# A modulation product moved out of the first attention unit, with its arithmetic spread over later groups

## The chip, the cores and the metric

The kernel runs on one core of a Trainium2 chip. The metric is the device time of one execution in microseconds; lower is better. The engines are named as in the profile: PE is TensorE (matrix products), with PEld for its weight loads; DVE is VectorE, ACT is ScalarE, POOL is GpSimd, and SP is the engine whose queue issues most of the DMAs. Each engine works through its own queue in program order and waits on semaphores for the others.

## The reference

It is one transformer block with adaptive layer norm. A small vector `c` per batch element yields six modulation rows, the attention is an ordinary softmax attention with 16 heads over 1024 tokens and 8 batch elements, and the second half is a mixture of eight experts, each of which picks its 512 best tokens.

```python
mod = (_silu(L0_c) @ L0_wmod).reshape(8, 6, 1, 256)
sa, ca, ga, sb, cb, gb = (mod[:, i] for i in range(6))
ga = (2 * (ga >= 0) - 1) * jnp.maximum(jnp.abs(ga), 0.25)
gb = (2 * (gb >= 0) - 1) * jnp.maximum(jnp.abs(gb), 0.25)
h = _layernorm(x) * (1 + ca) + sa
x = x + ga * attention(h, w_qkv, w_o)
h = _layernorm(x) * (1 + cb) + sb
x = x + gb * experts(h, router_w, router_b, w1, b1, w2, b2)
```

The change touches only `ga`, `sb`, `cb` and `gb`: they are needed late, at the end of the first batch element's attention, while `sa` and `ca` are needed at once.

## The kernel before

The attention is cut into 128 units (`NSU`): one unit is a batch element, a pair of heads and half of the queries. A unit has four groups, so the program runs through groups g = -1, 0, 1, 2, ... and unit u begins at group 4u. In every group PE computes two score products of the current unit into PSUM tiles `s` (L393); ACT copies them into SBUF tiles `p` (L402) and DVE keeps a running maximum `top` of them (L410). In the first group of the next unit (`gm == 0`) the finished maximum is turned: PE transposes `top` into the PSUM tile `tt` (`max_turn`, L420), DVE reduces it and splits it in three bfloat16 parts (`split_max`, L428 to L438), PE turns these into `pn` (`max_rows`, L444), ACT copies that to `nr` (L449), and a group later PE spreads it over all rows as `less` (`max_spread`, L457). DVE then subtracts it from the scores (L460), eight times a unit, ACT takes the exponentials (L463), PE multiplies with the values (L473, tile `av`), and POOL sums the exponentials for the denominators (L493, L496).

Everything else hangs as tasks at a group and a place in it. `at(g, where, f, *args)` registers a task, `run(g, where)` issues it. The order of the places in a group is: "load", "turn", the turn of the maximum, the score products and their copies, "post" (in a unit's first group it comes here, in other groups later), subtractions, "add" and "sum", maxima and the remaining subtractions, "m1", exponentials, products with the values (in a unit's first group `max_rows` stands among them or in their place), "pool", "m2". The schedule is manual: this program order is each engine's order.

In the first groups the query, key and value products (`qk_task` L352 with copies L357 and L363, `v_task` L373 with copy L378) are tasks at "m1". Their PSUM buffers come from `bank`, which hands out a list written by hand before it falls back on the single buffer "mm":

```python
    early = [(ps_s, "s")] * 2 + [(ps_m, "mm"), (ps_av, "av")] + [
        (ps_b, "less"), (ps_m, "mm"), (ps_av, "av")
    ] * 4
```

The buffer "less" also serves `tt` and `less`, "mm" also serves `pn`, and "av" the products with the values. Each of the three has one buffer, so a new tile in it waits until the tile before it has been read.

The modulation rows are made by `mod_rows(i)` for i = 0 and 1, each with four matrix products (L228) into a tile `pr` from `bank` and a copy by ACT into the tile `mrow` (L231), which has eight rows. The call with i = 1 goes on with the arithmetic on DVE (one addition, L234, and four operations for each of the two gates, L238 to L242) and stores the rows to DRAM by two DMAs on SP's queue (L243, L244). The calls are tasks at "m2" of groups 2 and 3. The tile `mrow` lies in the buffer "rb", of which there is one; its next taker is the spread denominator `rb` (`den_spread`), first loaded in group 21 for POOL's multiplication in group 22 (L558). The stored rows are first read from DRAM in group 30 (`gates`) and in group 80 (`out_load`).

Of the kernel before, what the change touches and what calls it, by code (L numbers as in the profile page):

```python
# [28 lines left out]
F32 = mybir.dt.float32  # L29
# [5 lines left out]
ALU = mybir.AluOpType  # L35
# [9 lines left out]
def adaln_block(  # L45
# [15 lines left out]
    nc = tc.nc  # L61
    B, S, D = x.shape
# [66 lines left out]
    small = attn.enter_context(tc.tile_pool(name="small", bufs=4))  # L129
# [68 lines left out]
    mod_row = []  # L198
# [22 lines left out]
    def mod_rows(i):  # L221

        if i == 0:
            mod_row.append(work.tile([B, 4 * D], F32, tag="rb", name="mrow", bufs=1))
        mrow = mod_row[0]
        pr = bank([B, 2 * D], f"pr{i}")
        for k in range(KC):
            nc.tensor.matmul(  # L228
                pr, sT[:, k, :], wm[1 + i][:, k, :], start=(k == 0), stop=(k == KC - 1)
            )  # L230
        nc.scalar.copy(mrow[:, 2 * i * D : (2 * i + 2) * D], pr)  # L231
        if i == 0:
            return
        nc.vector.tensor_scalar_add(mrow[:, 2 * D : 3 * D], mrow[:, 2 * D : 3 * D], 1.0)  # L234
        for i in (0, 3):
            g = mrow[:, i * D : (i + 1) * D]
            sign = small.tile([B, D], F32, tag="ox", name=f"sign{i}", bufs=3)
            nc.vector.tensor_scalar(sign, g, 0.0, 2.0, op0=ALU.is_ge, op1=ALU.mult)  # L238
            size = small.tile([B, D], F32, tag="at", name=f"size{i}", bufs=2)
            nc.vector.scalar_tensor_tensor(size, g, -1.0, g, op0=ALU.mult, op1=ALU.max)  # L240
            nc.vector.tensor_scalar_max(size, size, 0.25)
            nc.vector.scalar_tensor_tensor(g, sign, -1.0, size, op0=ALU.add, op1=ALU.mult)  # L242
        nc.sync.dma_start(mod_d, mrow[:, : 3 * D])  # L243
        nc.sync.dma_start(gb_d, mrow[:, 3 * D :])  # L244

# [5 lines left out]
    def at(g, where, f, *args):  # L251
        steps.setdefault((g, where), []).append((f, args))
# [13 lines left out]
    def bank(shape, name):  # L266
        pool, tag = early.pop(0) if early else (ps_m, "mm")
        return pool.tile(shape, F32, tag=tag, name=name)
# [490 lines left out]
    for b in range(B):  # L759
# [17 lines left out]
        if b + 1 < B:  # L777
            for t in range(NT):
                g = 64 * (b + 1) + 18 + 8 * t
# [17 lines left out]
    for b in range(B):  # L797
        at(64 * b + 30, "load", gates, b)
    for i in range(2):
        at(2 + i, "m2", mod_rows, i)  # L800
    at(4 * NSU - 2, "load", last_mods)
    at(4 * NSU - 6, "load", last_load)
    at(4 * NSU + 4, "load", last_load_den, 0)
# [3 lines left out]
    with tc.manual_schedule():  # L807
# [15 lines left out]
        g = -1  # L823
# [172 lines left out]
    with tc.tile_pool(name="search", bufs=2) as se, tc.tile_pool(  # L996
        name="pos", bufs=1
    ) as po_, tc.tile_pool(name="se_ps", bufs=2, space=PSUM) as sps, tc.tile_pool(
        name="pos_ps", bufs=1, space=PSUM
    ) as pps:  # L1000
        for dst, pattern, mult in (
# [3 lines left out]
            i = po_.tile(list(dst.shape), I32, name=f"i_{dst.name}")  # L1005
# [324 lines left out]
```

## Time and profile before

| | us |
|---|---|
| median of 3 runs | 3397.42 (3396.98 to 3397.81) |
| profiled execution | 3399.97 |
| its span, first to last instruction | 3398.3 |
| PE busy | 3316.2 (98% of the span) |
| DVE busy | 2723.2 (80%) |
| POOL busy | 2702.0 (80%) |
| ACT busy | 2465.8 (73%) |
| mean granted PE clock | 0.987 |

The span is what the trace covers; the profiled execution's own time has 1.67 us more around it. Times in the views are microseconds from the start of the span. In the trace groups 2, 3, 4, 8, 12 and 16 begin on PE at 29.05, 36.33, 43.62, 68.84, 89.95 and 111.60 us. A regular unit thus takes about 21 to 22 us, and the attention takes most of the span. A line of a timeline gives the start, the duration, the engine, the source line and operation, what it writes and reads, how many instructions are merged into the line, and in brackets the idle time of the engine before it with whom it waited for.

### The profile page before, as it was taken

The page shows a single profiled execution, that of the slowest core. Times are in us where ns is not written, and L with a number is a line of the kernel's source. Part 1 is how long each engine was busy: PE and PEld are TensorE (multiplying, and loading weights), DVE is VectorE, ACT ScalarE, POOL GpSimd, SP SyncE. Part 2 cuts the span into 40 slices and gives each one's busy share as a digit, 9 for nine tenths or more (in the row PEclk, how much of TensorE's full clock was granted, in tenths as well). Part 3 has the DMA queues.
Part 4 walks back from the last instruction along what each step waited for, and adds up shares of the span by engine and source line. Part 5 has one row for each costly group of instructions (what it writes and reads, how often), then busy time and mean ns, then how long its engine had stood idle before and what let it go on. Part 6 is the DMA issues. An engine that isn't in the chain of part 4 may idle for free. (4 is left out here: it accounts for less than half of the span.)

```text
span 3398.3 us, 60059 instructions
## 1 busy us (share of the span) xinstructions
PE 3316.2 (98%) x23647; PEld 1345.2 (40%) x23647; DVE 2723.2 (80%) x3391; ACT 2465.8 (73%) x3069; POOL 2702.0 (80%) x1611
## 2 busy tenths in 40 slices
PE   8999999999999999999999999999999999985998
PEld 3333333333333333333333333333333333334666
DVE  6898888888888888888888888888888888876332
ACT  5888887778777877778777787878777787760221
POOL 2899888988898888989898888988898888881333
PEclk9999999999999999999999999999999999996999
DMA  4020012111121112111121112111211112124342
GB/s 82 14 48 30 26 48 53 45 46 53 45 63 42 47 53 56 43 46 51 48 59 42 47 53 56 49 40 51 61 46 48 42 51 60 51 76 140 105 102 44
DMA packets 184110, 183.66 MB, mean 54 GB/s; under 512 B 49148, under 2 KB 161292, under 8 KB 183700
## 3 DMA queue, kind: packets, MB, share of 16 engines
q1 hardware_dynamic: 167860, 158.44, 16.9%
q0 software_dynamic: 7168, 12.72, 1.9%
q10 hardware_dynamic: 8800, 8.68, 0.8%
q8 instruction: 185, 3.03, 0.4%
q14 instruction: 97, 0.79, 0.1%
HBM read 126.01 MB, written 62.16 MB: 55 GB/s over the span
## 5 line engine op out<-in xcount | busy, mean ns | idle before, releaser
L496 POOL TENSOR_TENSOR acc<-acc,p 128x1024 f32<-128x1024 f32 x764 | 1816.3, 2377 | 89.8 <-ACT p L463 42.3
L402 ACT COPY p<-s 128x1024 f32<-128x1024 f32 x1024 | 990.4, 1016 | 332.7 <-PE s L393 311.4
L460 DVE TENSOR_TENSOR p<-p,less 128x1024 f32<-128x1024 f32 x1024 | 1211.3, 1214 | 8.7 <-PE less L457 3.7
L410 DVE TENSOR_TENSOR top<-top,s 128x1024 f32<-128x1024 f32 x768 | 934.2, 1216 | 134.6 <-ACT p L402 120.1
L463 ACT ACTIVATE p<-p 128x1024 f32<-128x1024 f32 x1024 | 1025.4, 1052 | 1.4 <-DVE rd L695 1.0
L393 PE MATMUL s<-qk,qk 64*128 64x512 f32 (+1 forms) x6144 | 999.1, 603 | 3.2 <-DVE top L410 3.2
L473 PE MATMUL av<-p,v 128*64 128x512 f32 x4096 | 995.5, 596 | 1.6 <-ACT p L463 1.4
L352 PE MATMUL pq<-hT,wq 128*64 128x512 f32 x2048 | 497.3, 607 | 0.7 <-ACT hT L304 0.7
L393 PEld LDWEIGHTS s<-qk,qk 64*128 64x128 f32 (+1 forms) x6144 | 315.5, 151 | 418.1 <-issue 232.2
L473 PEld LDWEIGHTS av<-p,v 128*64 128x64 f32 x4096 | 270.6, 137 | 487.1 <-issue 387.6
L493 POOL TENSOR_TENSOR acc<-p,p 128x1024 f32<-128x1024 f32 x128 | 304.7, 2380 | 61.5 <-ACT p L463 61.5
L428 DVE TENSOR_REDUCE tt<-tt 128x8 f32<-128x1024 f32 x128 | 157.7, 1232 | 176.2 <-PE tt L420 176.2
L352 PEld LDWEIGHTS pq<-hT,wq 128*64 128x64 f32 x2048 | 124.9, 136 | 350.0 <-issue 219.4
L373 PE MATMUL pv<-wq,hT 128*64 128x256 f32 x2048 | 249.8, 386 | 0.0
L630 POOL TENSOR_TENSOR ox<-ox,at 128x256 f32<-128x256 f32 x56 | 40.6, 725 | 253.1 <-DVE at L625 253.1
L614 PE MATMUL po<-wo,ot 128*64 128x256 f32 x1792 | 202.9, 379 | 0.0
L373 PEld LDWEIGHTS pv<-wq,hT 128*64 128x64 f32 x2048 | 136.0, 137 | 156.8 <-issue 58.3
L410 DVE TENSOR_TENSOR top<-p,s 128x1024 f32<-128x1024 f32 x128 | 154.8, 1209 | 46.1 <-ACT p L402 42.8
L614 PEld LDWEIGHTS po<-wo,ot 128*64 128x64 f32 x1792 | 128.6, 137 | 88.7 <-issue 32.0
L558 POOL TENSOR_TENSOR oT<-oT,rb 128x1024 f32<-128x1024 f32 x63 | 150.1, 2382 | 0.0
L357 ACT ACTIVATE qk<-pq 128x512 f32<-128x512 f32 x128 | 76.5, 598 | 94.9 <-PE pq L352 94.9
L1264 POOL DMA_INDIRECT out_dram<-eo,tok x32 | 53.8, 1680 | 115.0 <-DMA out_dram<-eo,tok 61.4
(192 smaller groups left out, 2237.8 us busy)
## 6 DMA issues: line engine op xcount, KB each, us to landing
rb<-rden_d SPq DMA_DIRECT2D x126, 256.0 KB
oT_d<-oT SPq DMA_DIRECT2D x60, 512.0 KB
ot<-oT_d SPq DMA_DIRECT2D x56, 512.0 KB
rows_d<-gb_d SPq DMA_DIRECT2D x8, 1024.0 KB
w<-in_L_ffn_w_dram SPq DMA_DIRECT2D x8, 1024.0 KB
w<-in_L_ffn_w_dram ACTq DMA_DIRECT2D x8, 1024.0 KB
rows_d<-row SPq DMA_DIRECT2D x62, 132.0 KB
lnx<-in_L_attn_inputs_dram SPq DMA_DIRECT2D x28, 256.0 KB
```

Of the source, the lines that this page charges most:

```text
L352: nc.tensor.matmul(pq[m * N : (m + 1) * N, :], wq_of(k, a, 2 * p + m), hTs[b][:, k, sl], start=(k == 0), stop=(k == KC - 1),)
L373: nc.tensor.matmul(pv[m * N : (m + 1) * N, i, :], hTs[b][:, k, t0 : t0 + N], wq_of(k, 2, 4 * g, 4), start=(k == 0), stop=(k == KC - 1),)
L393: nc.tensor.matmul(ps[k : k + n, j, :], kt[r, c * P + k : c * P + k + n], qt[r, h * QB : (h + 1) * QB], start=True, stop=True,)
L402: nc.scalar.copy(probs[u, c], ps)
L410: nc.vector.tensor_tensor(tops[u], probs[u, 0] if c == 1 else tops[u], ps, ALU.max)
L428: nc.vector.tensor_reduce(nm[:, 0, :], tt.rearrange("p r q k -> p q r k"), AX.XY, ALU.max, negate=True)
L460: nc.vector.tensor_tensor(probs[u, c], probs[u, c], less[u], ALU.add)
L463: nc.scalar.activation(probs[u, c], probs[u, c], AF.Exp)
L473: nc.tensor.matmul(avs[u][j * N : (j + 1) * N, :], v[:, c, hh * N : (hh + 1) * N], pT[:, j, :], start=(c == 0), stop=(c == NT - 1),)
L493: nc.gpsimd.tensor_tensor(sums[u], pts[0], pts[1], ALU.add)
L496: nc.gpsimd.tensor_tensor(sums[u], sums[u], pt, ALU.add)
L614: nc.tensor.matmul(po[m * N : (m + 1) * N, :], ot[:, p, m * N : (m + 1) * N], wo[:, p, :], start=(p == 0), stop=(p == NP - 1),)
```

## The change

The two calls of `mod_rows` move from "m2" of groups 2 and 3 to group 4, the first group of the second unit: the call with i = 0 to "m1" (before `max_rows`), the one with i = 1 to "m2" (after it). The arithmetic of the gates becomes `mod_gate`, called at "post" of groups 8 and 12, and the addition with the two stores becomes `mod_store`, called at "post" of group 16. All of these are first groups of a unit, where "post" stands ahead of the subtractions and maxima. The number of instructions stays the same.

```diff
@@ mod_rows
         nc.scalar.copy(mrow[:, 2 * i * D : (2 * i + 2) * D], pr)
-        if i == 0:
-            return
+
+    def mod_gate(i):
+        g = mod_row[0][:, i * D : (i + 1) * D]
+        sign = small.tile([B, D], F32, tag="ox", name=f"sign{i}", bufs=3)
+        nc.vector.tensor_scalar(sign, g, 0.0, 2.0, op0=ALU.is_ge, op1=ALU.mult)
+        size = small.tile([B, D], F32, tag="at", name=f"size{i}", bufs=2)
+        nc.vector.scalar_tensor_tensor(size, g, -1.0, g, op0=ALU.mult, op1=ALU.max)
+        nc.vector.tensor_scalar_max(size, size, 0.25)
+        nc.vector.scalar_tensor_tensor(g, sign, -1.0, size, op0=ALU.add, op1=ALU.mult)
+
+    def mod_store():
+        mrow = mod_row[0]
         nc.vector.tensor_scalar_add(mrow[:, 2 * D : 3 * D], mrow[:, 2 * D : 3 * D], 1.0)
-        for i in (0, 3):
-            g = mrow[:, i * D : (i + 1) * D]
-            sign = small.tile([B, D], F32, tag="ox", name=f"sign{i}", bufs=3)
-            nc.vector.tensor_scalar(sign, g, 0.0, 2.0, op0=ALU.is_ge, op1=ALU.mult)
-            size = small.tile([B, D], F32, tag="at", name=f"size{i}", bufs=2)
-            nc.vector.scalar_tensor_tensor(size, g, -1.0, g, op0=ALU.mult, op1=ALU.max)
-            nc.vector.tensor_scalar_max(size, size, 0.25)
-            nc.vector.scalar_tensor_tensor(g, sign, -1.0, size, op0=ALU.add, op1=ALU.mult)
         nc.sync.dma_start(mod_d, mrow[:, : 3 * D])
         nc.sync.dma_start(gb_d, mrow[:, 3 * D :])
@@ the tasks
     for i in range(2):
-        at(2 + i, "m2", mod_rows, i)
+        at(4, ("m1", "m2")[i], mod_rows, i)
+        at(8 + 4 * i, "post", mod_gate, 3 * i)
+    at(16, "post", mod_store)
```

## The prediction

> **What bounds the kernel now.** I read the page first: TensorE (PE) is busy for 98% of the span and its slices are flat until the tail, so a change pays only where it takes time off PE's path. The chain that ended last reaches back only over the last microseconds and says nothing of the start.
>
> ```profile
> span 3398.3 us, 60059 instructions
> PE 3316.2 (98%) x23647; PEld 1345.2 (40%) x23647; DVE 2723.2 (80%) x3391; ACT 2465.8 (73%) x3069; POOL 2702.0 (80%) x1611
> ```
>
> Second, the windows view over the first units (columns: window, length, busy us of PE, PEld, DVE, ACT, POOL, granted clock, DMA share, GB/s). PE is full from 20 to 44 us, has a hole in 44 to 49, and runs at half clock from there to about 55.3. Unit 2 (69 to 90) is full again.
>
> ```profile
> 36.00:44.00 8.00, 8.00 (x57) 2.80 (x58) 2.44 (x2) 3.96 (x6) 0.00 (x0) 1.00 0.00 1
> 44.00:49.00 5.00, 2.10 (x20) 0.79 (x16) 4.42 (x13) 2.23 (x3) 0.00 (x0) 1.00 0.05 10
> 49.00:51.00 2.00, 1.02 (x11) 0.81 (x13) 1.31 (x3) 0.58 (x1) 0.00 (x0) 0.50 0.00 0
> 51.00:53.00 2.00, 2.00 (x8) 1.00 (x6) 1.74 (x2) 0.03 (x1) 0.00 (x0) 0.50 0.00 0
> 53.00:55.00 2.00, 2.00 (x6) 0.35 (x6) 1.60 (x2) 1.30 (x2) 0.00 (x0) 0.50 0.00 0
> 69.00:90.00 21.00, 21.00 (x132) 6.67 (x130) 19.22 (x20) 17.87 (x22) 16.46 (x8) 1.00 0.00 1
> ```
>
> Third, PE's timeline there (start, length, operation, idle before and its releaser). Both products of the modulation rows (pr) are on a full PE. After the turn of the running maximum (tt) and two scores, PE waits 3.19 us for VectorE's `parts`.
>
> ```profile
> 34.52 1.88 PE L228 MATMUL pr<-wm,sT 128*8 128x512 f32 x4
> ...
> 39.99 1.89 PE L352 MATMUL pq<-hT,wq 128*64 128x512 f32 x8
> 41.80 1.88 PE L228 MATMUL pr<-wm,sT 128*8 128x512 f32 x4
> 43.62 0.71 PE L420 MATMUL tt<-ident,top 64*128 64x64 f32 x16
> 44.17 1.93 PE L393 MATMUL s<-qk,qk 64*128 64x512 f32 x8
> 49.30 0.64 PE L444 MATMUL pn<-ident_b,parts 128*64 128x128 bf16 x8 [3.19 <-DVE parts L438]
> 50.62 0.61 PE L457 MATMUL less<-nr,three 64*128 64x512 bf16 x2 [0.68 <-ACT nr L449]
> 51.00 3.64 PE L393 MATMUL s<-qk,qk 64*128 64x512 f32 x8
> ```
>
> Fourth, VectorE's timeline says why `parts` is late: the modulation arithmetic stands before the reduction in its queue and holds it until 47.14.
>
> ```profile
> 44.33 0.28 DVE L234 TENSOR_SCALAR mrow<-mrow 8x256 f32<-8x256 f32 x1 [3.26 <-ACT mrow L231]
> ...
> 46.80 0.41 DVE L242 SCALAR_TENSOR_TENSOR mrow<-sign,size 8x256 f32<-8x256 f32 x1
> 47.14 1.21 DVE L428 TENSOR_REDUCE tt<-tt 128x8 f32<-128x1024 f32 x1
> ```
>
> **The change, part by part.** I follow the edges on the profiled clock until tt of group 8 (68.84 before), where the pipeline is in its regular step.
>
> *Products out of groups 2 and 3.* Each costs PE its pitch: 34.52 to 36.33 and 41.80 to 43.62, 3.63 us together. ScalarE (about 3.1 us of work in such a group) and VectorE (2.54) have room in the 5.45 us left, so tt could start at 39.99.
>
> *A new wait there.* `bank` hands out a written list of PSUM buffers; two calls less before the third group's tasks move each later taker on by one. The last v product takes "av", and the query product of group 3 takes "less", the buffer that tt needs. Its copy by ScalarE ran 41.92 to 42.52; 1.81 earlier that is 40.11 to 40.71, and tt starts at 40.77, not 39.99. Behind tt in PE's queue stand the scores. That is 2.85 us earlier than before.
>
> *Arithmetic out of VectorE's way.* The reduction starts 0.75 after tt (68.84 to 69.59 in the next unit), at 41.52, and `parts` is done 2.16 later (47.14 to 49.30): 43.68.
>
> *Products into group 4.* PE: scores 41.32 to 43.18 (0.55 and 1.86 after, as at 43.62), the first product from 43.18, ended 45.06. It lies in "mm", which pn wants next, so pn waits for ScalarE's copy (0.05 and 0.58, the rows of L231): 45.75. So only some 0.5 us of the first product fill the wait for `parts`; the rest and the copy delay pn by 2.07. It is still 3.55 earlier than 49.30. The second product ("av", free since group 3) starts a warm pn pitch later (0.23, from 72.16 to 72.39): 45.98 to 47.80. It covers the copy nr (done about 46.8). So less starts at 47.80 (50.62 before). Its own copy of 0.58 on ScalarE ends at about 48.4, before the next scores are there at 49.0.
>
> *Unit 1 after that.* VectorE starts subtracting 0.43 after less (73.35 to 73.78): 48.23. Its eight subtractions and six maxima took 16.11 us without gaps in unit 2 (73.78 to 89.89), and 17.53 in unit 1 (51.26 to 68.79), where the half clock made scores late. With the clock up they end at 64.34, and tt starts at 64.40. PE's own work of 14.8 us from 47.80, with its waits for score buffers, ends near 64.2. Gain at group 8: 68.84 - 64.40 = 4.44 us.
>
> *The clock.* The row: 3.19 us of idle PE was followed by a granted 0.50 until about 55.3, and scores took 3.64 instead of 1.88. The two waits I add (0.78 and 0.75) are nearest to the 0.53 us one at 64.12, in a stretch granted 1.00, so I take no drop. The other bound: one drop like that of before, priced by its rows as 1.76 (scores), 0.69 (v, pitch 2.47 against 1.78) and 0.47 (pn, less), 2.9 us in all.
>
> The Trainium skill, "TensorE: Matmul & The Clock Gate", Part 1, puts the drop after an idle window of about 3.4 us that runs free of the kernel. Read strictly it would have spared the 3.19 us gap, and the regained clock time (estimate 1.4 us of the gain, 17.53 - 16.11) would not exist, so the gain at group 8 would be 3.0; the row shows the drop, and the row decides.
>
> *Gates into groups 8 and 12.* Four operations each, 1.30 us by their pitch (44.54 to 45.84). They stand behind the reduction and before the first maximum of the group. Before, VectorE idled 0.81 there for ScalarE's copy, so 0.49 sticks out. In unit 2 VectorE ended at 89.89 and PE's tt followed at 89.95: no slack, so 0.49 is lost, for the maximum frees score buffers and then tt. In unit 3 the subtraction had 0.1 to spare and tt came at 111.60, 0.49 after VectorE's end at 111.11; the remaining 0.4 disappears. Without these covers both gates cost 2.6.
>
> *The add and the two stores in group 16.* One 0.28 us operation in the same 0.81 gap: nothing, or 0.2 if that gap is gone. SP waits for it now from the denominator store of group 13 on; behind it are the next denominator store (group 17) and the load of group 19. The rows are first read from DRAM in group 30. `mrow` shares its single buffer with rb, loaded in group 21; before, rb's issue was at 137.84 against group 16's 111.60, some 26 us later, so nothing.
>
> Sum: -4.44 + 0.49 = -3.95 us, which stays to the end because PE is full from there (its waits from 100 to 2900 us are 7.3 us in all). The profiled execution lasted 3399.97 us (span 3398.3 and 1.67 around it), so it would last 3396.0. It lies 2.55 above the median of the three runs, 3397.42; the same difference gives 3393.5 us.
>
> **The rivals.**
>
> - *The clock falls anyway*, since two short waits come within 6 us. Then 2.9 comes back: -1.0, 3396.4 us. For it: half clock after a hole is what the trace shows. Against: the hole was four times as long.
> - *The gates are not covered.* Both fully on VectorE's path, with the add: -4.44 + 2.6 + 0.2 = -1.6, 3395.8 us. For it: unit 2 has no slack. Against: the 0.81 us gaps, and unit 3's 0.49.
> - *Slower: the shared buffer.* mrow is now held until its two stores from group 16 have landed, and rb cannot be loaded before. GpSimd's multiplication at 146.67 waits for rb, the sums queue behind it, they release the probability tiles, and PE stands. It decides once the stores take more than the 26 us of room; from there each microsecond costs up to one. For a result 6.8 us slower they must take about 37 us: 26 of room, 4 of gain and 6.8. Against: the small store of the denominators, issued at 136.27, was followed by the load that reads it at 137.84. Price then 3404.2 or more.
> - *Faster by more than the start can give.* Even with PE without a gap unit 1 cannot gain over 4.6. PE's 27 waits of L512 for VectorE's L677 come to 9.1 us; if a shifted phase took half, the sum would be about -8.5, 3389 us. Against: they come from the order inside a unit, which does not move.
>
> **How the numbers follow.** Forecast 0.68, clock 0.10, gates 0.08, shared buffer 0.06, outside gain 0.08. A measurement of this kernel tells about 0.2% (6.8 us) from no change. The first three lie inside it: same 0.86; faster 0.08; slower 0.06. The likeliest time is 3393.5. Its terms give 3392 to 3395; the range reaches up over the gates' and the clock's cases (3396.6), and down to 3391.2, as if neither new wait nor the gate cost anything (0.78, 0.49) and a further microsecond were found at the buffers. Outside stay the last two rivals and little else.
>
> **What would show it.** Right: tt of group 4 near 40.8 with a wait of some 0.8 for the query copy; pn near 45.75 released by ScalarE's copy of mrow, not by `parts`; clock 1.00 over 44 to 57; tt of group 8 near 64.4, of group 12 near 86.0, of group 16 near 107.65; the regular units unchanged. Wrong: a half clock after 46, a wait of tt in groups 12 or 16 for VectorE over 1 us, a wait of rb for mrow's stores, or a difference that arises after 130 us.

## The result, and the profile after

The changed kernel is slower: 3411.08 us (median of 6 runs, 3410.15 to 3412.42) against 3397.59 us of before on the same chip, a ratio of 1.0038 (95% interval 1.0028 to 1.0047). The forecast was 3393.5 us, with a range from 3391.2 to 3396.6. The page's header shows most of the loss as time without PE work: in the profiled executions the span grew by 12.4 us, PE's busy time by 3.0.

```profile
span 3410.7 us, 60057 instructions
PE 3319.2 (97%) x23647; PEld 1345.2 (39%) x23647; DVE 2737.8 (80%) x3391; ACT 2466.4 (72%) x3069; POOL 2701.9 (79%) x1611
```

PE's timeline has what was forecast for groups 4 to 8: the two small new waits, the turn of group 4 released by the query copy, pn released by the copy of `mrow`, no half clock. After that it has two waits of 5.6 and 5.7 us for VectorE that were not forecast.

```profile
41.36 0.71 PE L422 MATMUL tt<-ident,top 64*128 64x64 f32 x16 [0.70 <-ACT qk L359]
46.32 0.41 PE L446 MATMUL pn<-ident_b,parts 128*64 128x128 bf16 x8 [0.66 <-ACT mrow L231]
...
65.09 0.72 PE L422 MATMUL tt<-ident,top 64*128 64x64 f32 x16
...
76.46 2.08 PE L395 MATMUL s<-qk,qk 64*128 64x512 f32 x4 [5.61 <-DVE top L412]
...
106.09 2.08 PE L395 MATMUL s<-qk,qk 64*128 64x512 f32 x4 [5.72 <-DVE top L412]
```

VectorE's timeline in group 8 names the cause. These are the same four gate operations as before, with the same shapes. Three of them last 2.17, 2.31 and 2.53 us instead of 0.27, 0.28 and 0.41. The first maximum of the group starts only at 75.20. Before, in group 4:

```profile
45.84 0.27 DVE L238 TENSOR_SCALAR sign<-mrow 8x256 f32<-8x256 f32 x1
46.04 0.41 DVE L240 SCALAR_TENSOR_TENSOR size<-mrow 8x256 f32<-8x256 f32 x1
46.48 0.28 DVE L241 TENSOR_SCALAR size<-size 8x256 f32<-8x256 f32 x1
46.80 0.41 DVE L242 SCALAR_TENSOR_TENSOR mrow<-sign,size 8x256 f32<-8x256 f32 x1
```

After, in group 8:

```profile
67.86 2.17 DVE L236 TENSOR_SCALAR sign<-mrow 8x256 f32<-8x256 f32 x1
69.95 0.41 DVE L238 SCALAR_TENSOR_TENSOR size<-mrow 8x256 f32<-8x256 f32 x1
70.40 2.31 DVE L239 TENSOR_SCALAR size<-size 8x256 f32<-8x256 f32 x1
72.75 2.53 DVE L240 SCALAR_TENSOR_TENSOR mrow<-sign,size 8x256 f32<-8x256 f32 x1
75.20 1.20 DVE L412 TENSOR_TENSOR top<-p,s 128x1024 f32<-128x1024 f32 x1
```

GpSimd's timeline in narrow windows gives its single additions beside that. One ran from 67.51 to 69.88, the next from 69.96 to 72.57, the last from 72.65 to 75.00. Each long VectorE operation ends 0.14 to 0.28 us after the end of one of these additions. The one gate operation that stayed short (69.95 to 70.36) began with the 69.96 addition, and that addition is the one stretched, to 2.61 us from the usual 2.37.

```profile
67.51 2.37 POOL L498 TENSOR_TENSOR acc<-acc,p 128x1024 f32<-128x1024 f32 x1
...
69.96 2.61 POOL L498 TENSOR_TENSOR acc<-acc,p 128x1024 f32<-128x1024 f32 x1
...
72.65 2.35 POOL L498 TENSOR_TENSOR acc<-acc,p 128x1024 f32<-128x1024 f32 x1
```

The starts of tt (us) give the account group by group:

| group | before | forecast | after | after less before |
|---|---|---|---|---|
| 4 | 43.62 | 40.77 | 41.36 | -2.26 |
| 8 | 68.84 | 64.40 | 65.09 | -3.75 |
| 12 | 89.95 | 86.0 | 94.61 | +4.66 |
| 16 | 111.60 | 107.65 | 123.67 | +12.07 |
| 20 | 133.22 | not given | 146.04 | +12.82 |

The shortfall against the forecast at group 4, 0.6 us, was there before any changed instruction: the first scores began at 18.64 instead of 18.03. From group 20 to the end of the span the difference stays (+12.4).

### The profile page after: what moved, and what is told of

It reads as the page before. It is cut to its first block, busy times and chain, and to the rows that moved or that the text cites. A ratio compares the mean times of both kernels' runs of the same rounds, so it can differ in the third digit from the quotient of the medians.

```text
span 3410.7 us, 60057 instructions
## 1 busy us (share of the span) xinstructions
PE 3319.2 (97%) x23647; PEld 1345.2 (39%) x23647; DVE 2737.8 (80%) x3391; ACT 2466.4 (72%) x3069; POOL 2701.9 (79%) x1611
## 5 line engine op out<-in xcount | busy, mean ns | idle before, releaser
L462 DVE TENSOR_TENSOR p<-p,less 128x1024 f32<-128x1024 f32 x1024 | 1212.1, 1215 | 10.1 <-PE less L459 5.4
```

The source lines that it names most:

```text
L462: nc.vector.tensor_tensor(probs[u, c], probs[u, c], less[u], ALU.add)
```

## The experiments

Three theories. **Port**: VectorE and GpSimd share a way into SBUF that one instruction holds from its start to its end, so a small VectorE operation of certain forms waits out a whole GpSimd addition. **Wait**: the operations wait for something that their new place or the products' new place brings, such as a buffer or a semaphore. **Share**: GpSimd's traffic slows VectorE's in proportion. Each time below stands beside the kernel before, run on the same chip: 3398.45 us in the first four experiments, 3398.54 in the last four.

**products_only.** The arithmetic follows the second product at once:

```diff
         at(4, ("m1", "m2")[i], mod_rows, i)
-        at(8 + 4 * i, "post", mod_gate, 3 * i)
-    at(16, "post", mod_store)
+    for i in range(2):
+        at(4, "m2", mod_gate, 3 * i)
+    at(4, "m2", mod_store)
```

> Both products of the modulation rows in group 4 as in the changed kernel, but the nine arithmetic operations and the stores stay right behind the second product, in group 4 on VectorE, where GpSimd has not begun to work (its first addition came at 59.7 before). Theory 'port': the small operations are held only while GpSimd works on SBUF, so here they take 0.27 to 0.41 us each, 2.8 in all. They stand before the subtractions of unit 1 and make them 3.1 us later than in the changed kernel (52.0 instead of 48.9); tt of group 8 near 68.3, up to 69.5 if PE's wait in group 5 halves the clock; the regular units unchanged; 3397 us, within 1.5. Theory 'wait' (the operations wait for something that the new place of the products brings, a buffer or a semaphore): they take over 2 us again, 3405 or more. Theory 'share' (GpSimd slows VectorE's SBUF traffic in proportion): as 'port' here.

Measured: 3397.0 us, ratio 0.9996 (0.9987 to 1.0006), no measurable difference. VectorE's timeline has every small operation short again.

```profile
45.79 0.28 DVE L236 TENSOR_SCALAR sign<-mrow 8x256 f32<-8x256 f32 x1
...
49.64 0.41 DVE L240 SCALAR_TENSOR_TENSOR mrow<-sign,size 8x256 f32<-8x256 f32 x1
```

tt of group 8 came at 66.34, not 68.3: the first gate fitted into VectorE's wait for `less`, which I had not counted. Groups 8 to 16 took the regular 21.12 and 21.65. The loss is not in the products.

**pool_quiet.** GpSimd leaves out six additions in each of three units:

```diff
-        else:
+        elif u not in (1, 2, 3):
             for pt in pts:
                 nc.gpsimd.tensor_tensor(sums[u], sums[u], pt, ALU.add)
```

> The changed kernel without GpSimd's six additions into the sum in each of the units 1, 2 and 3 (left out: three quarters of these three units' denominators), so that GpSimd is idle while the gates are computed in groups 8 and 12 and while the addition of group 16 runs. Theory 'port': the operations return to 0.27, 0.41, 0.28 and 0.41 us; tt of groups 8 to 12 and 12 to 16 in 21.6 us each instead of 29.5 and 29.1; about 3394 us, 17 below the changed kernel. Theory 'wait': durations over 2 us and 3411 us as in the changed kernel. Theory 'share': as 'port' here.

Measured: 3401.84 us, ratio 1.0010 (1.0000 to 1.0020), 8 us above the expected time. I had overlooked that the additions running in group 8 belong to unit 0, which was not silenced. Groups 8 to 12 therefore took 29.47 us. So the two gates of one run became the comparison. In group 8, beside the additions, the gate was held as before; in group 12, beside an idle GpSimd, it was not. VectorE's timeline of this kernel:

```profile
67.41 2.16 DVE L236 TENSOR_SCALAR sign<-mrow 8x256 f32<-8x256 f32 x1
...
72.29 2.52 DVE L240 SCALAR_TENSOR_TENSOR mrow<-sign,size 8x256 f32<-8x256 f32 x1
...
96.88 0.27 DVE L236 TENSOR_SCALAR sign<-mrow 8x256 f32<-8x256 f32 x1
...
97.83 0.41 DVE L240 SCALAR_TENSOR_TENSOR mrow<-sign,size 8x256 f32<-8x256 f32 x1
```

The second gate has the same instructions at the same place, so "wait" falls. Groups 12 to 16 took 21.64 us (94.11 to 115.75) instead of 29.06.

**gates_on_pool_late.** The gates, written with five operations instead of four, and the addition run on GpSimd, in groups 8, 12 and 16:

```diff
-        nc.vector.tensor_scalar(sign, g, 0.0, 2.0, op0=ALU.is_ge, op1=ALU.mult)
+        nc.gpsimd.tensor_scalar(sign, g, 0.0, 2.0, op0=ALU.is_ge, op1=ALU.mult)
+        nc.gpsimd.tensor_scalar(sign, sign, 1.0, 1.0, op0=ALU.subtract, op1=ALU.mult)
...
-        nc.vector.scalar_tensor_tensor(size, g, -1.0, g, op0=ALU.mult, op1=ALU.max)
-        nc.vector.tensor_scalar_max(size, size, 0.25)
-        nc.vector.scalar_tensor_tensor(g, sign, -1.0, size, op0=ALU.add, op1=ALU.mult)
+        nc.gpsimd.tensor_tensor(size, g, sign, ALU.mult)
+        nc.gpsimd.tensor_scalar(size, size, 0.25, 1.0, op0=ALU.max, op1=ALU.mult)
+        nc.gpsimd.tensor_tensor(g, sign, size, ALU.mult)
...
-        nc.vector.tensor_scalar_add(mrow[:, 2 * D : 3 * D], mrow[:, 2 * D : 3 * D], 1.0)
+        nc.gpsimd.tensor_scalar(
+            mrow[:, 2 * D : 3 * D], mrow[:, 2 * D : 3 * D], 1.0, 1.0, op0=ALU.add, op1=ALU.mult
+        )
```

> The changed kernel with the gates (five operations each) and the addition computed by GpSimd instead of VectorE, in the same groups 8, 12 and 16. Theory 'port': GpSimd does not contend with itself, and VectorE's remaining operations read at most one SBUF operand, so nothing is held: VectorE's regular pace, PE without the waits of 5.6 and 5.7 us, about 3394 us. GpSimd has 4 us or more of room in a unit for some 3 us of small operations. Theory 'wait': what held the operations holds GpSimd now, with over 2 us each, and the sums come late: 3397 to 3405. Theory 'share': as 'port', with small operations slower on GpSimd.

Measured: 3393.35 us, ratio 0.9984 (0.9975 to 0.9994). With the arithmetic on the other engine the change gains. PE's timeline has tt at 64.40, 85.52 and 107.17 in groups 8, 12 and 16, with the regular steps of 21.12 and 21.65 and no wait for VectorE in groups 8 to 16. GpSimd has room for a gate of some 5 us:

```profile
63.51 1.10 POOL L236 TENSOR_SCALAR sign<-mrow 8x256 f32<-8x256 f32 x1
...
67.81 0.73 POOL L241 TENSOR_TENSOR mrow<-sign,size 8x256 f32<-8x256 f32 x1
```

**pool_halves.** GpSimd's additions of units 1 to 3 are cut in two:

```diff
+        elif u in (1, 2, 3):
+            for pt in pts:
+                for j in range(2):
+                    nc.gpsimd.tensor_tensor(sums[u][:, j], sums[u][:, j], pt[:, j], ALU.add)
         else:
```

> The changed kernel with GpSimd's additions of units 1, 2 and 3 cut in two, 128x512 instead of 128x1024 each, about 1.25 us instead of 2.37, the same work in twice as many instructions. Theory 'port', with the port held for a whole GpSimd instruction: VectorE's three held operations of a gate wait for one short addition each, so they take about 1.2 us instead of 2.2 to 2.5, a gate 4 us instead of 7.3, and the loss of 15 us shrinks by 6 to 8: 3403 to 3405 us. Theory 'share': the traffic of GpSimd is the same, so durations and time stay as in the changed kernel, 3411. Theory 'wait': 3411.

Measured: 3406.16 us, ratio 1.0024 (1.0014 to 1.0033). Group 8, beside unit 0's whole additions, was held as before; in group 12 the held operations shrank with the instruction they wait for:

```profile
96.66 1.19 DVE L236 TENSOR_SCALAR sign<-mrow 8x256 f32<-8x256 f32 x1
97.77 1.49 DVE L238 SCALAR_TENSOR_TENSOR size<-mrow 8x256 f32<-8x256 f32 x1
...
100.56 1.37 DVE L240 SCALAR_TENSOR_TENSOR mrow<-sign,size 8x256 f32<-8x256 f32 x1
```

GpSimd moved the same bytes, so "share" falls: the wait goes with the length of the instruction. The time saved was 5 us rather than 6 to 8, for two reasons. The first gate had whole additions beside it, so groups 8 to 12 still took 29.34 us; groups 12 to 16 took 25.40 instead of 29.06. And in group 12 all four operations were held, so that this gate took 5.2 us, not the expected 4 (7.4 in the changed kernel).

**arithmetic_only_late.** The products return to groups 2 and 3:

```diff
-        at(4, ("m1", "m2")[i], mod_rows, i)
+        at(2 + i, "m2", mod_rows, i)
         at(8 + 4 * i, "post", mod_gate, 3 * i)
```

> The products stay at the end of groups 2 and 3 as before; only the arithmetic and the stores go to groups 8, 12 and 16 on VectorE. Theory 'port' (the held operations are the whole loss, and the products' place is worth little): tt of group 4 back at 43.6, but VectorE free for the reduction, so pn near 46.5 and less near 47.8, tt of group 8 near 64.4, as early as in the changed kernel; then the same held operations (2.2 to 2.5 us) and 3411 us, within 2 of the changed kernel. Rival 'products' (moving the products gave most of the 3.7 us of gain): tt of group 8 near 68, and 3414 to 3415.

Measured: 3410.62 us, ratio 1.0035 (1.0022 to 1.0049), the changed kernel's loss without its moved products. tt of group 8 came at 64.37, as early as with them (65.09 in the changed kernel, 64.40 in gates_on_pool_late).

**products_kept_pool_arithmetic.** Products in groups 2 and 3, arithmetic on GpSimd (written as in gates_on_pool_late) right behind them:

```diff
-        at(4, ("m1", "m2")[i], mod_rows, i)
-        at(8 + 4 * i, "post", mod_gate, 3 * i)
-    at(16, "post", mod_store)
+        at(2 + i, "m2", mod_rows, i)
+    for i in range(2):
+        at(3, "m2", mod_gate, 3 * i)
+    at(3, "m2", mod_store)
```

> The products stay in groups 2 and 3; the arithmetic goes to GpSimd, directly behind the second product in group 3, where GpSimd is otherwise idle until about 55. Theory 'port': nothing is held, VectorE reduces at once, tt of group 8 near 64.4 and the regular units unchanged: 3393 to 3394, as with the gates on GpSimd in groups 8 and 12. Rival 'products': tt of group 8 near 67 to 68 and 3396 to 3397.

Measured: 3393.47 us, ratio 0.9986 (0.9976 to 0.9995), tt of group 8 at 64.61. So the gain of the change comes from taking the arithmetic out of the reduction's way; with the written list of buffers as it was, moving the products adds nothing that can be seen (3393.47 against 3393.35 us).

**pool_arithmetic_other_buffers.** The version meant to beat both, on the GpSimd variant:

```diff
-    ] * 4
+    ] * 2 + [(ps_b, "less"), (ps_m, "mm")] * 2 + [(ps_av, "av"), (ps_m, "mm"), (ps_av, "av")]
...
-        at(4, ("m1", "m2")[i], mod_rows, i)
-        at(8 + 4 * i, "post", mod_gate, 3 * i)
-    at(16, "post", mod_store)
+        at(4 + i, ("m1", "m2")[i], mod_rows, i)
+        at(4 + i, "m2", mod_gate, 3 * i)
+    at(5, "m2", mod_store)
```

> A version meant to beat both: first product in group 4 ahead of max_rows but in the buffer av, second product in group 5 in av, the written list changed so that the query product of group 3 keeps mm and the last v product keeps less; the arithmetic on GpSimd right behind each product. Both new waits of PE (0.70 for the query copy, 0.66 for the copy of mrow) should be gone, tt of group 4 near 40.1, less near 45.5, VectorE's 16.1 us from there, tt of group 8 near 62.2: 2.2 us under the version with the gates on GpSimd in groups 8 and 12, so 3391 us against 3397.5 of before. If PE's score buffers set unit 1 instead, 3392 to 3393.

Measured: 3391.41 us, ratio 0.9978 (0.9969 to 0.9987), the lowest median of all. Its interval overlaps those of the two versions before it on GpSimd, but tt of group 8 is 2 us earlier than theirs. Both new waits are gone in PE's timeline, and of PE's waits in groups 4 to 8 only the 0.80 us one for `nr` is left:

```profile
40.35 0.71 PE L425 MATMUL tt<-ident,top 64*128 64x64 f32 x16
...
45.79 0.39 PE L462 MATMUL less<-nr,three 64*128 64x512 bf16 x2 [0.80 <-ACT nr L454]
...
62.45 0.71 PE L425 MATMUL tt<-ident,top 64*128 64x64 f32 x16
```

**probe_forms.** The kernel before with one more small operation, after a memset, in each of the units 6 to 13, in four forms:

```diff
+        nc.vector.memset(a, 1.0)
+        if k % 4 == 0:
+            nc.vector.tensor_scalar(b, a, 0.0, 2.0, op0=ALU.is_ge, op1=ALU.mult)
+        elif k % 4 == 1:
+            nc.vector.scalar_tensor_tensor(b, a, -1.0, a, op0=ALU.mult, op1=ALU.max)
+        elif k % 4 == 2:
+            nc.vector.tensor_tensor(b, a, a, ALU.mult)
+        else:
+            nc.vector.reciprocal(b, a)
...
+        at(24 + 4 * k, "post", probe, k)
```

> The kernel before with one added small operation on VectorE (8x256, after a memset of its input) in the first group of units 6 to 13, in turn a tensor_scalar, a scalar_tensor_tensor with two SBUF inputs, a tensor_tensor with two SBUF inputs and a reciprocal, while GpSimd adds. Theory 'port', as the Trainium skill words it ('SBUF — State Buffer', Who interferes with whom): tensor_scalar and the two forms with two SBUF inputs are held up to the end of a GpSimd addition, 0.3 to 2.6 us by their moment, the reciprocal and the memset never, near 0.3 us. Theory 'small operations' (whatever is short and on eight partitions is held): the reciprocal and the memset over 2 us too.

One run, 3405.74 us. VectorE's timeline:

```profile
157.08 0.27 DVE L805 MEMSET prs<- 8x256 f32 x1
157.38 1.90 DVE L807 TENSOR_SCALAR prd<-prs 8x256 f32<-8x256 f32 x1
...
179.91 1.88 DVE L809 SCALAR_TENSOR_TENSOR prd<-prs 8x256 f32<-8x256 f32 x1
...
203.36 0.94 DVE L811 TENSOR_TENSOR prd<-prs 8x256 f32<-8x256 f32 x1
...
226.23 1.74 DVE L813 RECIPROCAL prd<-prs 8x256 f32<-8x256 f32 x1
```

GpSimd's addition beside the first pair ran from 156.76 to 159.13: the memset inside it was not held, the tensor_scalar ended 0.15 after it. The tensor_tensor ended at 204.30, 0.28 after an addition that began at 201.66 and took 2.36.

```profile
156.76 2.37 POOL L496 TENSOR_TENSOR acc<-acc,p 128x1024 f32<-128x1024 f32 x1
```

All eight memsets lay inside additions and took 0.27 us; the second operation of each of the three held forms again ended 0.15 to 0.28 us after an addition's end. So "small operations" as a cause falls by the memset. The reciprocal was far from the expected 0.3 us, but not held either: both took exactly 1741 ns, though one began 0.28 us before the end of an addition and the other 1.3 us before. That 1741 ns is its own speed is thus likely; no run shows one beside an idle GpSimd.

## Why the prediction was wrong

The step that failed is the price in "Gates into groups 8 and 12": "Four operations each, 1.30 us by their pitch (44.54 to 45.84)". That row came from group 4, when GpSimd had not started. The prediction's own windows lines show the difference: POOL is busy 0.00 us in 44 to 49 and 16.46 of the 21 us in 69 to 90. In group 8 the gate took 7.34 us (67.86 to 75.20), in group 12 7.45 (97.38 to 104.83), because three of its four operations each waited for the end of a GpSimd addition. In place of the 0.49 us that was to stick out in unit 2, and to disappear in unit 3, the units lost 8.41 and 7.41. The same error sits in the add of group 16: 2.28 us instead of 0.28, and tt of group 20 lost 0.75 more. A price taken from a stretch where a neighbour is idle is no price for a stretch where it is busy.

What the runs show is that such an operation ends just after the GpSimd instruction beside it. No run shows by itself what the two engines contend for. The Trainium skill states the rule that I missed: "SBUF — State Buffer", Who interferes with whom, says that VectorE and GpSimd share one pair of SBUF ports as an exclusive lock, which a VectorE instruction wants when it runs in a two-port mode (tensor_scalar can) or has two SBUF inputs. This case agrees: the held operations of the gates took 2.15 to 2.53 us beside additions of 2.37, 1.19 to 1.49 beside additions of half the width, and the same operations 0.27 to 0.41 beside none. VectorE's regular operations here read one operand from PSUM; the subtractions (L462) took 1.20 to 1.22 us inside a GpSimd addition as outside one.

From 6 us of holding to the measured loss, in unit 2. The maximum began 10.11 us after tt (65.09 to 75.20) instead of 3.69 (68.84 to 72.53): 6.42. The line of before:

```profile
72.53 1.22 DVE L410 TENSOR_TENSOR top<-p,s 128x1024 f32<-128x1024 f32 x1 [0.81 <-ACT p L402]
```

PE waited 5.61 for its score buffer, and the hole halved its clock, as the windows view shows (PE's clock is the third value from the right).

```profile
76.00:78.00 2.00, 1.54 (x4) 0.50 (x4) 2.00 (x3) 0.00 (x0) 0.00 (x0) 0.50 0.00 0
78.00:80.00 2.00, 2.00 (x6) 0.53 (x6) 2.00 (x3) 1.01 (x1) 0.00 (x0) 0.50 0.00 0
...
82.00:94.00 12.00, 12.00 (x72) 3.44 (x70) 10.23 (x10) 10.20 (x13) 7.06 (x3) 1.00 0.00 0
```

The late and slowed PE made scores late, and VectorE waited 1.67 us for their copy.

```profile
86.00 1.22 DVE L412 TENSOR_TENSOR top<-top,s 128x1024 f32<-128x1024 f32 x1 [1.67 <-ACT p L404]
```

From the first maximum to the last took 19.00 us (75.20 to 94.20) instead of 17.36, another 1.64, and tt followed VectorE's end by 0.41 instead of 0.06: 0.35. Together 8.41, the difference of 29.52 and 21.11. Unit 3 lost 7.41 in the same way (29.06 against 21.65).

Point by point. The wait for "less" (0.78 forecast, 0.70) and for "mm" (0.75, 0.66) came as described. So did unit 1: from tt of group 4 to tt of group 8, 23.63 forecast and 23.73 measured, though inside it PE's own work from less to tt was 15.4 us, not 14.8, and its wait for a score buffer 1.17, not some 1.6. PE stayed at full clock through 44 to 57 as taken; it fell only in the 5.6 us hole. The half clock of before lasted a little longer than read, to between 55.5 and 56 instead of about 55.3; no sum uses that.

Calling the products' move a part of the gain was loose: arithmetic_only_late and products_kept_pool_arithmetic reach the same group 8 without it. Without its 0.49 us for the gates the forecast's sum is 4.44 us of gain, and it held where VectorE has no gates: in gates_on_pool_late tt comes 4.44 us earlier in group 8 (64.40) and 4.43 in group 16 (107.17), and its time is 5.1 us lower (2 to 8.5 by its interval). That the first figure agrees to the hundredth is luck: the first scores began 0.09 us earlier there than before. The bound "unit 1 cannot gain over 4.6" was none: it is 68.84 - 64.2, from PE's path with its waits for score buffers, and pool_arithmetic_other_buffers has tt of group 8 6.39 us earlier (62.45).

The rival "The gates are not covered" had the right place and engine, but priced both gates at 2.6 us and the add at 0.2 where the rows give 14.8 and 2.3. The slower rival was wrong: SP sent the stores at 128.75 and 129.13, and units from group 20 on were regular. The clock rival's mechanism did appear, through a wait that I had not seen.

## What to carry to other kernels

Before moving work to "a place where the engine has room", look at what the other engine runs there: once GpSimd is busy, a 0.3 us operation of VectorE of the forms held here (tensor_scalar, scalar_tensor_tensor, tensor_tensor, all with their inputs in SBUF) costs up to one whole GpSimd instruction, and a chain of four cost three of them. Price a moved instruction by a row from the stretch it moves into, or keep both a quiet and a busy bound. The remedy was to give the small side arithmetic to GpSimd itself, which had the room, and to check the list of buffers whenever the order of its takers changes.

## What was not expected of the hardware

- The hold goes both ways: the VectorE operation that began together with a GpSimd addition stayed at 0.41 us and the addition took 2.61 us instead of 2.37. In these runs the one that began later is held: in all six gates beside whole additions this operation (L238) began 0.003 to 0.007 us ahead of the addition; in group 12 of pool_halves it began at 97.77, 0.11 us behind an addition, and took 1.49 us.

```profile
97.66 1.32 POOL L499 TENSOR_TENSOR acc<-acc,p 128x512 f32<-128x512 f32 x1
```

- On GpSimd a tensor_scalar of 8x256 took 1.06 to 1.10 us with is_ge, subtract or max ahead of the multiplication and 0.40 us with add ahead of it; a tensor_tensor of that size took 0.71 to 0.74.
